# Counting the edges of a graph with the digit built on VectorE, eight one-hots kept, and TensorE's products in one written order

## The chip, the cores and the metric

The kernel runs on one core of one Trainium2 chip. A core has five engines that this text names: TensorE (PE), which multiplies matrices; VectorE (DVE), ScalarE (ACT) and GpSimd (POOL), which work on rows; and SyncE (SP), which here only issues transfers. Each runs its own queue of instructions in order, and semaphores join them. TensorE writes its sums to eight banks of PSUM; VectorE and ScalarE copy them out to SBUF, the memory in which the operands lie. The metric is the device time of one execution in microseconds (us).

## What is computed

The reference is a chain of four residual layers on 625 nodes of 512 features. Only the first is touched by the change: a graph convolution in hyperbolic space, done twice with two sets of weights. Cut to what matters:

```python
x = x + L0_gnn(layernorm(x), edge_index, W1, b1, W2, b2)   # this layer
x = x + L0_ffn(layernorm(x), ...)                           # eight experts, top 2
x = x + L1_gnn(layernorm(x), ...)                           # a second graph layer
x = x + L1_ffn(layernorm(x), ...)                           # memory attention, gated map

def gcn_conv(x, W, b, row, col, norm, n):
    h = mobius_matvec(W, x)              # x @ W.T, then scaled by its norms
    h = mobius_add(h, expmap0(b))
    t = logmap0(h)
    msg = norm[:, None] * t[row]
    agg = segment_sum(msg, col, num_segments=n)
    return expmap0(agg)                  # tanh(norm) * u / norm, kept inside the ball
```

There are 10,000 edges and a loop at each node. `norm` is the product of both ends' degrees to the power -0.5.

## The kernel before

The nodes are held as 5 tiles of 125 rows (`NT`, `P`). The sum over the edges is a product with a dense matrix AT of 625 x 625 counts, made once and used in both convolutions and again in the third layer.

**The count.** The 10,000 edges lie as 80 columns of 125. For each column VectorE compares the numbers 0 to 624 with the edges' senders (`sh`, L355, 125 x 625 in f16) and the numbers 0 to 374 with their receivers (`at_node`, L356, 125 x 375). A receiver of 375 or above is counted in the same 375 columns with a weight of 4096, so that one sum holds two digits. ScalarE multiplies that weight in (`dh`, L357). TensorE then adds `sh` times `dh` to five banks (`eps`, L361, five products a column; the fifth has a row of ones more, whose sums are the degrees). `sh` rotates over three tiles (`NSH`), `dh` over three, `at_node` over two. The function `count_edges` (L343 to L399) does this for a group of columns: 0 to 15 (`EARLY`), 16 to 47, 48 to 79 (`GROUP` is 32). At a group's end VectorE copies the degree sums (`total`, L370), TensorE turns them (`dps`, L373), ScalarE copies the five banks as integers (`both`, L386), and VectorE splits the digits (L390) and adds them to AT (L395; ScalarE writes the first group's, L393). The last group's degrees give `dis`, the root of their inverse.

**The nodes.** VectorE takes the statistics of x (L228, L231), ScalarE the root, and VectorE writes the normalised rows `u` (L244). The statistics are ordered behind the sixth column (`AHEAD`). ScalarE squares `u` for its norms (L255). In `conv_in` (L407) TensorE turns the weights (`wps`, L414) and `u` (`trps`, L265), ScalarE and VectorE copy these out (`WT` L415, `uT` L267 and L269), and TensorE makes five map tiles of 125 x 512 (`mxps`, L438). Of each tile ScalarE takes the squares (L440), VectorE the product with the bias row `yb` (L442), and ScalarE a copy (`raw`, L444). A chain of small operations on VectorE and ScalarE follows, with four changes of ScalarE's function table (L99), and at last a scaling of `raw` (L484, L485). `conv_out` (L488) scales by `dis` and makes the aggregation `agps` (L496, 25 products of 125 x 512), and so on for the second weights.

**What sets the order.** A scheduler at compile time places each engine's instructions by the order of the program and their expected readiness; tiles of a pool rotate over their buffers, and the eight banks are one pool (`psum`, L290) in this layer. `order(later, sooner)` (L187) puts one instruction behind another of its engine. `busy` (L193) issues fills: products of `full` with itself whose results nobody reads; there are 18 ahead of the second aggregation (L492) and 31 ahead of the first turn of the second layer's rows (`trps` at L568, in that layer's own pool of banks, L549). At the start SP, ACT and POOL each issue a part of the loads of indices, x, weights and bias; the first weights of the experts are issued on SP once the statistics have read x (`nodes_in`, L519, L630).

Of the kernel before, what the change touches and what calls it, by code (L numbers as in the profile page):

```python
# [16 lines left out]
F32 = mybir.dt.float32  # L17
# [32 lines left out]
EARLY = 16  # L50

AHEAD = 6

NSH = 3
# [4 lines left out]
def rows_of(ap, n):  # L59

    return bass.AP(tensor=ap.tensor, offset=ap.offset, ap=[[0, n], [1, ap.shape[-1]]])


class Rows:
# [42 lines left out]
    def artanh(self, out, z):  # L107
# [14 lines left out]
        self.chain(out, ln, 0.5, s, OP.mult, OP.add)  # L122
    def norm(self, n, inv, sq):

        self.act(n, sq, AF.Sqrt)
        self.at_least(n, n, EPS)
        self.inverse(inv, n)

    def expmap0(self, sq, name):
# [3 lines left out]
        n, inv = self.new("ex_n"), self.new("ex_inv")  # L133
        scale, inside = self.new(name + "_s"), self.new(name + "_n")
        self.norm(n, inv, sq)
# [7 lines left out]
def layers_kernel(  # L143
# [49 lines left out]
    def busy(ps, n, behind):  # L193

        for _ in range(n):
            filled = T.matmul(ps[:, :128], full, full, start=True, stop=True)
            order(filled, behind)
# [39 lines left out]
    def layernorm(y, extra=None, behind=None, pieces=((0, NT),)):  # L237
# [10 lines left out]
        return read  # L248
# [9 lines left out]
    def transposed(psum, to, y, c, scale=1.0, pieces=PIECES, wait=None):  # L258

        for a, b in pieces:  # L260
            ps = psum.tile([128, 512], F32, tag="ps", name="trps")
            if wait is not None and a == 0:
                busy(ps, *wait)
            for t in range(a, b):
                T.transpose(ps[:, (t - a) * P : (t - a + 1) * P], y[:, t, c * 128 : (c + 1) * 128], ident[:P, :P])  # L265
# [14 lines left out]
    with ExitStack() as es:  # L280
        big = spool(es, "l0big", 1)
        work = spool(es, "l0work", 2)
        hot = spool(es, "hot", 3)
# [29 lines left out]
        senders = [big.tile([P, N + 1], F16, name=f"sh_{i}") for i in range(NSH)]  # L313
# [29 lines left out]
        def count_edges(first, last):  # L343
# [5 lines left out]
            acc = [psum.tile([128, 512], F32, tag="ps", name="eps") for _ in range(NT)]  # L349
            rows_of_acc = [P] * (NT - 1) + [P + 1]  # L350
            for j in range(first, last):
                sh = senders[j % NSH]
                at_node = hot.tile([P, HALF], F16, tag="at", name="at_node", bufs=2)
                dh = hot.tile([P, HALF], F16, tag="dh", name="dh")
                V.tensor_scalar(sh[:, :N], nodes, src_f[:, j : j + 1], None, op0=OP.is_equal)  # L355
                built = V.tensor_scalar(at_node, nodes[:, :HALF], dst_f[:, j : j + 1], None, op0=OP.is_equal)  # L356
                A.activation(dh, at_node, AF.Copy, scale=weight[:, j : j + 1])  # L357
                if j == AHEAD - 1:
                    ahead.append(built)
                for i, n in enumerate(rows_of_acc):  # L360
                    T.matmul(acc[i][:n, :HALF], sh[:, i * P : i * P + n], dh, start=j == first, stop=j == last - 1)  # L361
            digits = ((0, HALF, OP.bitwise_and, DIGIT - 1), (HALF, N - HALF, OP.logical_shift_right, SHIFT))
            both = work.tile([P, NT, HALF], I32, tag="both", name="both", bufs=1)
            with ExitStack() as now:
                if last == EC:
                    now.enter_context(tc.high_priority())


                total = big.tile([128, NT * D], F32, tag="uT" if first else "raw", name="total")[: P + 1, :HALF]
                V.tensor_copy(total, acc[NT - 1][: P + 1, :HALF])  # L370
# [14 lines left out]
            for i in range(NT):  # L385
                A.activation(both[:, i, :], acc[i][:P, :HALF], AF.Copy)  # L386
# [20 lines left out]
        def conv_in(k, u, scale, inside, pieces, own=None):  # L407


# [6 lines left out]
            yb = work.tile([P, D], F32, tag="yb", name="yb", bufs=1)  # L416
            V.tensor_scalar(yb, b_row[k], b_scale[:, k : k + 1], None, op0=OP.mult)
            y2 = b_square[:, k : k + 1]

            uT = big.tile([128, NT * D], F32, tag="uT", name="uT")[:, : DC * N].rearrange("p (c n) -> p c n", n=N)  # L420
# [906 lines left out]
```

## Time and profile before

| | us |
|---|---|
| median of 3 runs (2324.1 to 2325.33) | 2324.68 |
| the profiled execution | 2322.8 |
| its span, from the first to the last instruction | 2320.8 |
| PE busy in the span | 2232.5 (96%) |
| VectorE busy | 1621.8 (70%) |
| ScalarE busy | 867.1 (37%) |
| first product of the count starts at | 5.88 |
| first product of the first map (L438) starts at | 43.99 |
| first product of the first aggregation (L496) starts at | 133.62 |
| first turn of the second layer's rows (L265) starts at | 222.84 |

Times are from the span's start. An engine that is busy for 96% of the whole span may still stand idle in a stage, so the table is to be read beside the windows that the prediction shows. A busy PE may also run at a granted clock below 1.00; the windows give that clock. The length that the profile gives for a short instruction has its latency in it: two instructions of VectorE that follow one another may start closer together than the length of the first, so starts are compared where a pace is meant. The profile's line numbers are those of the listing above.

### The profile page before, as it was taken

How to read it: one execution, taken by the hardware profiler on the slowest of the kernel's cores; microseconds unless marked ns; L12 is line 12 of the kernel's file. 1: busy time of each engine (PE TensorE's matmuls, PEld its weight loads, DVE VectorE, ACT ScalarE, POOL GpSimd, SP SyncE). 2: the span in 40 equal slices, each digit the busy share in tenths (PEclk: the TensorE clock that was granted, in tenths of full speed). 3: DMA queues.
4: the chain of work that ended last, by engine and by line, in shares of the span. 5: the costliest groups of instructions: out<-in, count | busy, mean ns of one | idle time of the engine just before them, and what ended most of it. 6: DMA issues, size and time to landing. Idle time of an engine off the chain costs nothing.

```text
span 2320.8 us, 34522 instructions
## 1 busy us (share of the span) xinstructions
PE 2232.5 (96%) x12794; PEld 1768.9 (76%) x12794; DVE 1621.8 (70%) x2303; ACT 867.1 (37%) x2867; POOL 991.9 (43%) x1058
## 2 busy tenths in 40 slices
PE   6898999999999999999999999999999999999987
PEld 4655866665788888888888888888888888888853
DVE  5744533332477788888778888778888877888782
ACT  6755211111243434433433443343443343344322
POOL 1000000020146555666555566655566655556531
PEclk8999999999999999999999999999999999999989
DMA  7000588863123322222322222332222232221110
GB/s 254 1 8 29 192 290 291 301 209 78 32 39 95 74 59 59 65 59 71 87 69 59 66 59 59 94 74 59 59 66 59 68 91 68 59 66 40 42 59 22
DMA packets 326025, 204.67 MB, mean 88 GB/s; under 512 B 275534, under 2 KB 279563, under 8 KB 321000
## 3 DMA queue, kind: packets, MB, share of 16 engines
q1 hardware_dynamic: 317371, 189.65, 27.7%
q10 hardware_dynamic: 3639, 7.56, 0.9%
q0 software_dynamic: 4848, 5.26, 0.8%
q8 instruction: 101, 1.65, 0.3%
q14 instruction: 66, 0.54, 0.1%
HBM read 197.18 MB, written 5.23 MB: 87 GB/s over the span
## 4 chain that ended last, share of the span: by engine, by line
PE 86%; ACT 5%; DVE 4%; POOL 2%; issue 2%; DMA 1%; POOLq 0%; ACTq 0%; SPq 0%; DVEq 0%
PE h1ps L1135 35%; PE scps L1036 19%; PE kbps L1023 5%; PE hps L737 5%; PE ops L748 5%; PE zps L1072 3%; POOL zsq L1079 2%; PE eps L361 2%; ACT zs L1075 2%; PE stps L831 2%; PE agps L496 2%; PE atps L1063 2%; PE l1ps L838 1%; PE mxps L438 1%; DVE hacc L1183 1%
## 5 line engine op out<-in xcount | busy, mean ns | idle before, releaser
L1147 DVE TENSOR_TENSOR hacc<-hacc,h1ps 128x942 f32<-128x942 f32 (+1 forms) x510 | 529.0, 1084 | 11.7 <-PE h1ps L1135 11.7
L1036 PE MATMUL scps<-keys,xnT 128*125 128x400 f32 x1280 | 435.1, 499 | 0.0
L1095 POOL TENSOR_TENSOR wq<-wz 128x256 f32<-128x256 f32 x248 | 241.1, 982 | 405.6 <-PE h1ps L1135 347.4
L1036 PEld LDWEIGHTS scps<-keys,xnT 128*125 128x125 f32 x1280 | 240.0, 188 | 185.0 <-issue 3.8
L1044 ACT ACTIVATE att<-att,a_top 125x100 f32<-125x100 f32 x640 | 232.0, 364 | 361.5 <-DVE a_top L1039 361.5
L1135 PE MATMUL h1ps<-zT,wq 128*128 128x157 f32 x1736 | 302.8, 296 | 0.0
L1135 PE MATMUL h1ps<-zq,wq 128*128 128x157 f32 x1736 | 302.7, 297 | 0.0
L1079 POOL TENSOR_TENSOR zsq<-zsq,zs 128x628 f32<-128x628 f32 x124 | 187.6, 1513 | 201.5 <-ACT zs L1075 201.5
L1135 PEld LDWEIGHTS h1ps<-zT,wq 128*128 128x128 f32 x1736 | 256.2, 190 | 0.0
L1135 PEld LDWEIGHTS h1ps<-zq,wq 128*128 128x128 f32 x1736 | 255.9, 190 | 0.0
L1066 ACT ACTIVATE attT<-atps 100x375 f32<-100x375 f32 (+1 forms) x256 | 92.5, 432 | 397.4 <-PE atps L1063 397.4
L1095 POOL TENSOR_TENSOR wq<-wz,wq 128x256 f32<-128x256 f32 x248 | 210.9, 850 | 19.4
L1076 DVE TENSOR_SCALAR zT<-zps,cols 128x628 f32<-128x628 f32 x128 | 111.6, 872 | 149.0 <-ACT zs L1075 147.6
L1055 ACT ACTIVATE att<-att,a_tot 125x100 f32<-125x100 f32 x620 | 170.2, 364 | 10.7 <-DVE a_tot L1045 10.7
L1072 PE MATMUL zps<-attT,vc 100*128 100x314 f32 x512 | 161.0, 436 | 10.6 <-ACT attT L1066 10.5
L1095 POOL TENSOR_TENSOR wq<-wsum,wq 128x256 f32<-128x256 f32 x186 | 161.5, 868 | 14.6
L1095 POOL TENSOR_TENSOR wq<-wsum 128x256 f32<-128x256 f32 x186 | 135.9, 731 | 65.0 <-PE h1ps L1135 65.0
L1135 PE MATMUL h1ps<-zT,wz 128*128 128x157 f32 x992 | 152.6, 296 | 0.0
L1014 DVE STREAM_TRANSPOSE wqT<-wqraw 128x512 f32<-128x512 f32 x128 | 80.2, 681 | 101.6 <-PE kbps L1023 82.5
L1135 PEld LDWEIGHTS h1ps<-zT,wz 128*128 128x128 f32 x992 | 141.0, 190 | 9.1
L1075 ACT ACTIVATE zs<-zps 128x628 f32<-128x628 f32 x128 | 88.7, 693 | 124.7 <-POOL zsq L1079 111.2
L1072 PEld LDWEIGHTS zps<-attT,vc 100*128 100x128 f32 x512 | 87.5, 191 | 45.9 <-ACT attT L1066 26.9
(400 smaller groups left out, 3487.3 us busy)
## 6 DMA issues: line engine op xcount, KB each, us to landing
w<-in_L_ffn_w_dram SPq DMA_DIRECT2D x16, 4096.0 KB
wz<-in_L_ffn_wz_w_dram SPq DMA_DIRECT2D x32, 2048.0 KB
wqraw<-in_L_ffn_Wq_w_dram SPq DMA_DIRECT2D x512, 64.0 KB
cb<-qbias SPq DMA_DIRECT2D x32, 195.3 KB
wkv<-in_L_ffn_Wkv_w_dram SPq DMA_DIRECT2D x1, 4096.0 KB
W_raw<-in_L_gnn_W_dram SPq DMA_DIRECT2D x2, 1024.0 KB
w<-in_L_ffn_Wkv_w_dram SPq DMA_DIRECT2D x1, 2048.0 KB
l1w<-in_L_gnn_W_dram SPq DMA_DIRECT2D x2, 1024.0 KB
```

The costliest lines, as they stand in the source:

```text
L737: T.matmul(ps[:, i * CAP : (i + 1) * CAP], w1[e][:, c, hc * 128 : (hc + 1) * 128], xgT[e][:, c, :], start=c == 0, stop=c == DC - 1)
L748: T.matmul(ps[:CAP], hT[e][:, hc, :], w2[e][:, hc, :], start=hc == 0, stop=hc == HC - 1)
L1023: folded.last = T.matmul(ps[:, k, h * L : (h + 1) * L], wqT[b][h][:, (c + k) * 128 : (c + k + 1) * 128], kcT[:, b * HB // H, :], start=Tru ...
L1036: T.matmul(ps[:P, t - t0, : HB * L], xnT[:, c, tp(t)], keys[b][:, c, :], start=c == 0, stop=c == DC - 1)
L1044: A.activation(own, own, AF.Exp, bias=top[:, t, h : h + 1], accum_out=tot[:, t, h : h + 1])
L1055: A.activation(own, own, AF.Copy, scale=tot[:, t, h : h + 1])
L1072: T.matmul(ps[:, u, : 2 * QN], vc[:, g * DH : (g + 1) * DH], attT[h % 2][:, 2 * u * QN : 2 * (u + 1) * QN], start=True, stop=True)
L1075: A.activation(zs, ps[:, :, : 2 * QN], AF.Square)
L1079: nc.gpsimd.tensor_tensor(zsq, zsq, zs.rearrange("p u s -> p (u s)"), op=OP.add)
L1095: engine.tensor_tensor(to, x, y, op=OP.subtract)
L1135: T.matmul(ps[:, at % 6 // 3, at % 3 * QN : (at % 3 + 1) * QN], now[j][:, m * 128 : (m + 1) * 128], zquarter[b][j][:, place[i]], start=Tru ...
L1147: V.tensor_tensor(to, to, got, op=OP.add)
```

## The change

The count is cut into three parts: `counting` takes the banks, `column` builds one column and issues its five products, `taken` copies a group's sums out, and `added` splits them and adds them to AT. In the new order of the program:

- The groups are columns 0 to 31, 32 to 63 and 64 to 79. Nine fills stand ahead of the first column.
- VectorE builds `dh` in one operation: the comparison, and the multiplication by the weight. `at_node` and ScalarE's part are gone. `sh` and `dh` rotate over eight tiles each (`HOT`).
- 18 columns (`EARLY`) come ahead of the nodes' work, and the statistics are ordered behind the twelfth (`AHEAD`).
- The other 14 columns of the first group come between the five tiles of the first map, three behind each.
- A group's sums are taken at its end and added behind the second column of the next; the turns of the small vectors (`colps`, `gtps`) move from behind the count into the second group.
- Through all of this `T` is a `Lane`: each product is ordered behind the one before it in the program, so TensorE keeps the written order.
- The norms of `u` come from its variance in two small operations on VectorE, in place of ScalarE's squares. The scale of the bias is carried by two small operations and `yb` is gone.
- `u`, `uT` and `raw` rotate over two buffers in place of one for each.
- The 31 fills move from the turn of the second layer's rows to the end of the second `conv_out`, behind its last product and in a bank of this layer.

The diff, cut to its core:

```diff
-EARLY = 16
-AHEAD = 6
-NSH = 3
+EARLY = 18
+AHEAD = 12
+HOT = 8
...
+class Lane:
+    def __init__(self, engine, order):
+        self.engine, self.order, self.last = engine, order, None
+    def _behind(self, op):
+        if self.last is not None:
+            self.order(op, self.last)
+        self.last = op
+        return op
+    def matmul(self, *args, **kinds):
+        return self._behind(self.engine.matmul(*args, **kinds))
...
-                at_node = hot.tile([P, HALF], F16, tag="at", name="at_node", bufs=2)
-                V.tensor_scalar(sh[:, :N], nodes, src_f[:, j : j + 1], None, op0=OP.is_equal)
-                built = V.tensor_scalar(at_node, nodes[:, :HALF], dst_f[:, j : j + 1], None, op0=OP.is_equal)
-                A.activation(dh, at_node, AF.Copy, scale=weight[:, j : j + 1])
+            V.tensor_scalar(sh[:, :N], nodes, src_f[:, j : j + 1], None, op0=OP.is_equal)
+            built = V.tensor_scalar(dh, nodes[:, :HALF], dst_f[:, j : j + 1], weight[:, j : j + 1],
+                                    op0=OP.is_equal, op1=OP.mult)
...
-                    V.scalar_tensor_tensor(junk, ps[:P], 1.0, yb, op0=OP.mult, op1=OP.mult,
+                    V.scalar_tensor_tensor(junk, ps[:P], 1.0, b_row[k], op0=OP.mult, op1=OP.mult,
                                            accum_out=dot[:, t : t + 1])
                     A.activation(raw[:, t, :], ps[:P], AF.Copy)
+                    if beside is not None:
+                        beside(t)
...
+            if last:
+                product = busy(psum.tile([128, 512], F32, tag="ps", name="spare"), 31, product)
...
-        count_edges(0, EARLY)
-        u = big.tile([P, NT, D], F32, tag="u", name="u", bufs=1)
-        nodes_in = layernorm(u, behind=ahead[0])
-        s, inside = RP[0, NT].expmap0(squares(work, u, "in_sq"), "ex")
+        T = Lane(nc.tensor, order)
+        group = counting(0, GROUP)
+        busy(group[2][0], 9, None)
+        for j in range(EARLY):
+            column(group, j)
+        u = rotating("u")[:P].rearrange("p (t n) -> p t n", n=D)
+        mv, nodes_in = layernorm(u, behind=ahead[0])
...
+        V.tensor_tensor(sq, mv[:, :, 1], layernorm.rs, op=OP.mult)
+        r.chain(sq, sq, float(D), layernorm.rs, OP.mult, OP.mult)
...
-        sent, mapped = conv_in(0, u, s, inside, ((0, NT),))
-        for first in range(EARLY, EC, GROUP):
-            count_edges(first, min(first + GROUP, EC))
+        turned = turned_in(0, u)
+        rest = iter(range(EARLY, GROUP))
+        def beside(t):
+            for j in range(3):
+                for c in rest:
+                    column(group, c)
+                    break
+        sent, mapped = conv_in(0, turned, s, inside, ((0, NT),), beside=beside)
+        for j in rest:
+            column(group, j)
+        sums = taken(group)
+        for first in range(GROUP, EC, GROUP):
+            last = min(first + GROUP, EC)
+            group = counting(first, last)
+            for j in range(first, last):
+                column(group, j)
+                if j == first + 1:
+                    added(sums)
+                if j == first + 8 and first == GROUP:
...
+            sums = taken(group)
+        added(sums)
+        T = nc.tensor
...
-                transposed(psum, xfT[:, c, :], xf, c, pieces=(piece,), wait=None if c else (31, product))
+                transposed(psum, xfT[:, c, :], xf, c, pieces=(piece,), wait=None if c else (0, product))
```

## The prediction, written before the result was known

> **What bounds the kernel now.** I read the windows of 5 us first (where TensorE, PE, stands still), then PE's timeline (what ended each gap), then the groups by form (the length of one instruction). Only the first layer, 0 to 225 us, is touched.
>
> Windows; columns: stretch and its length, busy time and count of PE, weight loads, VectorE, ScalarE (ACT), GpSimd, then PE's granted clock, DMA share, GB/s.
>
> ```profile
> 35.00:40.00 5.00, 0.54 (x3) 0.31 (x3) 3.02 (x20) 4.97 (x13) 0.00 (x0) 0.67 1.00 406
> 40.00:45.00 5.00, 1.69 (x3) 0.78 (x4) 1.87 (x9) 4.97 (x12) 0.00 (x0) 0.50 1.04 387
> 70.00:75.00 5.00, 1.22 (x7) 0.76 (x6) 4.02 (x22) 4.96 (x10) 0.00 (x0) 0.93 0.00 2
> 75.00:80.00 5.00, 3.30 (x11) 2.42 (x11) 4.02 (x10) 3.37 (x6) 0.00 (x0) 0.50 0.00 0
> 85.00:90.00 5.00, 5.00 (x34) 4.28 (x33) 3.78 (x13) 3.88 (x7) 0.00 (x0) 1.00 0.00 0
> ```
>
> From 35 to 45 and 70 to 75 us ACT is full and PE nearly empty; behind each hole PE runs at clock 0.50. From 85 to 90 PE itself is the limit.
>
> PE's timeline; columns: start, length, instructions, and in brackets the idle time before them with what ended it.
>
> ```profile
> 16.13 8.26 PE L361 MATMUL eps<-dh,sh 125*125 125x375 f16 x40 [5.18 <-DVE sh L355]
> 42.16 0.68 PE L265 MATMUL trps<-ident,u 125*128 125x125 f32 x2 [6.17 <-ACT WT L415]
> 43.99 18.90 PE L438 MATMUL mxps<-WT,uT 128*125 128x512 f32 x40 [1.15 <-ACT uT L267]
> 76.70 22.21 PE L361 MATMUL eps<-dh,sh 125*125 125x375 f16 x125 [4.12 <-ACT dh L357]
> 133.62 24.45 PE L496 MATMUL agps<-raw,AT 125*125 125x512 f32 x50
> 181.55 4.18 PE L196 MATMUL agps<-full 128*128 128x128 f32 x36
> 214.19 8.82 PE L196 MATMUL trps<-full 128*128 128x128 f32 x62 [5.89 <-DVE x L510]
> 222.84 2.30 PE L265 MATMUL trps<-ident,xf 125*128 125x125 f32 x20
> ```
>
> The stage that changes runs from the first edge product (5.88 us) to the first product of the first aggregation (133.62 us): 127.7 us. At full clock its PE work is 88.9: 80 columns of edges at 0.795 (from 112 to 127 us each column's build starts that far behind the last) 63.6; five map tiles at 3.43 (the starts of the square sums at 53.4 and 56.8) 17.2; 16 turns of weights 1.95; 20 turns of nodes at 0.125 2.5; degree products 3 x 0.68 = 2.0; the turns of small vectors some 1.6. The brackets from 5.88 to 133.62 add up to about 28 us of idle, and half clock behind them makes the other 10 or 11. So 38.8 us is the most that order can win here.
>
> **What the change removes and adds, part by part.**
>
> *One column.* Groups by form; columns: busy us, mean ns, idle before and its releaser.
>
> ```profile
> L357 ACT ACTIVATE dh<-at_node,weight 125x375 f16<-125x375 f16 x80 | 47.9, 608 | 27.5 <-PE eps L361 13.3 <-DVE at_node L356 13.1 <-DVE ln_st L228 1.0
> L355 DVE TENSOR_SCALAR sh<-nodes,src_f 125x625 f16<-125x625 f16 x80 | 30.6, 382 | 2.9 <-PE eps L361 2.7
> L356 DVE TENSOR_SCALAR at_node<-nodes,dst_f 125x375 f16<-125x375 f16 x80 | 25.3, 318 | 9.3 <-ACT dh L357 9.1
> ```
>
> The 47.9 us on ACT goes, and with it one handover per column. VectorE's two builds start 0.30 and 0.23 us behind one another when nothing holds them (4.58, 4.88, 5.10). The second now also multiplies by a per-row scalar. No row shows that form in f16. Lower bound: 0.23, the multiplication free. Upper bound: the two-input add of 375 f32 elements (L395), 0.46 from start to start. The nearest row is the two-scalar subtract-and-multiply of L244, 512 f32: 0.46 from start to start against 0.40 for the one-scalar L405, so the second scalar costs 0.06 and leaves the rate. I take 0.23 + 0.06 = 0.29, a column 0.59 (0.53 to 0.76), below PE's 0.795. VectorE stays ahead, by up to eight columns in place of three.
>
> *The start.* Nine fills (36 records of such fills take 4.18, so two records a fill: 2.1 us at full clock, twice that at half) run while the indices are loading, ahead of any column. Columns begin at 4.58 + 0.59 = 5.2, and 18 of them end on PE at about 5.2 + 18 x 0.795 = 19.5, where before VectorE stood in the first statistics, waiting for x until 14.50, with six columns built. Now 12 to 18 are built by then (4.58 + 18 x 0.59 = 15.2). The node chain: statistics and aggregates 5 x 0.75 from 15.4 to 19.2, root and reciprocal to 19.9 (one table load of 1.28 now lies in ACT's idle time), five rows of u at 0.46 to 22.2; before, 28.4. The squares of u on ACT (5 x 0.81) are replaced by two small VectorE operations and leave the path. PE turns W meanwhile (19.5 to 22; its load's traffic ends at about 21) and u at 22.2 + 2.5, with some 1.5 for three free banks and the last copy: the map starts at 26.3, before 43.99.
>
> *Map and columns.* In the written order five tiles and 14 columns follow one another: 17.2 + 11.1 = 28.3, end 54.6. ACT's three visits to a tile lie beside it; VectorE needs 14 x 0.59 + 5 x 0.69 = 11.7 of the 28.3 and builds eight columns ahead.
>
> *First group border.* Five banks hold sums, three rotate. The next group's fourth and fifth products need copies of `both` on ACT (0.39 each from start to start), but there the chain behind the map runs, with four table loads of 1.28; before, fillers on ACT got places in it at 66.75, 68.76, 71.08 and then 76.15. Lower bound: 0.5 (two copies at once); upper: 12, if the copies come behind the last scaling (3.06), with a cold clock. The nearest rows are the fillers at the first two places, 3.8 and 5.9 us behind the last map product; from the group's end at 54.6 that is 2 to 4. I take 4.0, with a part at half clock: 58.6.
>
> *The other 48 columns.* 32 x 0.795 + 0.7 + 1.2 (vector turns, now in midst of columns) = 27.3. VectorE has in this time the chain (some 4.5), its five scalings (3.4), digits, diagonal and degrees (4) and 24 to 32 columns (14 to 19): about as much as PE. I add 1.5 for columns that come late: 87.4. Second border, ACT free: 1.0. Then 16 columns, one set of degree products and 1.0 for the 6.6 us of digits and sums on VectorE: 12.7 + 0.7 + 1.0. End at 102.8. The last columns' end to the first aggregation was 133.62 - 129.03 = 4.6, with 0.45 of it a digit ahead of the degree copy, and vector turns in it that are now earlier: I take 4.1. First aggregation at 106.9, **26.7 us earlier**. It then starts as cold as before and costs the same 24.45. The edits of the bias (its scale carried by small operations, no `yb`) take 0.48 of VectorE off twice, covered by PE in both maps: nothing; uncovered, 0.5.
>
> *The last fills.* 31 fills waited for the residual's last read (5.89 idle), ran cold in 8.82, and kept PE until 222.84, though the normalised rows were there at 217.6 and 219.5. Put behind the last aggregation in a bank of the same layer, they run warm from 208.3 to 215.5 (62 x 0.116). The turns then end about 0.9 behind the last row, 220.4 to 220.7 in place of 225.07: **4.4 us**. Bounds: 0, if the two idle us make the clock fall and routing waits elsewhere, and 5.
>
> Queues: on SP the first expert loads wait for the last statistics (issued at 21.76, now about 19); no transfer is put ahead of another. The first three weight tiles were there by 52 us, long ahead of their use after 225, and later ones start when tiles come free, so the rest moves along with the layer.
>
> **Sum.** 26.7 + 4.4 = 31.1. The profiled execution took 2322.8 us (span 2320.8, 2.0 outside it): 2291.7. The median shown is 2324.68, so 1.9 more: **2293.6**.
>
> A row against a rule. From 30 to 32 us PE turned W and u at granted clock 1.00, behind 1.39 of idle. The Trainium skill (TensorE: Matmul & The Clock Gate, Part 4: PE-mode transpose) says that such turns do not count as busy to the clock. By that rule the map would start cold behind 5 us of turns; with the half window of 3.4 us that the page gives, an estimate of 1.7 us, it would be 2295.3. By the row it is 2293.6; the row decides.
>
> **Rivals.**
> *A: PE in one order waits behind ACT.* For it: four table loads in the chain and a filler as late as 76.15; one order means that no later column may pass. Against: fillers found earlier places. At its upper bound the border costs 12 + 2 for the cold clock in place of 4: 10 later, 2304; 0.17.
> *B: VectorE becomes the bound*, the second operation taking the 0.46 of L395. A column is 0.76; from 54.6 on VectorE needs 40 x 0.76 + 19.4 = 50, the first aggregation comes at 110, with the start 2 to 3 later 113: six later, 2300; 0.13.
> *C: slower.* The same second operation, far dearer. Some 58 columns lie on VectorE's path (18 before the map, 40 behind it), so each 0.1 us more in a column costs 5.8. B's 2300 is 25 below before; the sign turns at 0.76 + 25 / 58 = 1.19 for a column, 0.89 for the operation. At 1.0 for it the time is 2300 + 58 x 0.54 = 2331. For it: f16 with two scalars is not in the trace. Against: no VectorE row of 375 elements is above 0.55. 0.04.
> *D: the change does not do what it says*: the statistics come ahead of columns 12 to 17, and VectorE's queue holds back columns at the border, so that the gaps move and do not close. With 3 of the 31.1 left the time is 2322; 0.04.
>
> **How the numbers follow.** Forecast 0.62: 2293.6, A 0.17, B 0.13, C 0.04, D 0.04. Lower end: border at 0.5 and no late columns (5 us), tail and fills 2 better, 0.53 for a column (3 us): 2284. Upper end: A with the fills' gain at zero, 2304 + 4.4, and 2 for columns: 2311. A measurement tells 0.2% (4.6 us) from no change. Faster by more 0.92, within 0.04, slower 0.04.
>
> **What would show it.** In the profile after: no dh on ACT; the second build at a distance of 0.29; no clock under 0.9 between 10 and 95 us; the first mxps at about 26; the gap ahead of the 33rd column about 2 to 4 and its releaser `both`; first agps at about 107; fills at its end with no gap. I am wrong if the columns' pace is VectorE's (over 0.795 with PE waiting for dh), if one gap above 8 us stands at a border, or if stages behind 225 us do not simply come earlier.

## The result, and the profile after

The changed kernel took **2296.43 us** (median of 4 runs, 2293.93 to 2299.3), the kernel before 2325.01 beside it (4 runs, 2324.1 to 2326.89): ratio 0.9876, 95% interval 0.9859 to 0.9894, 28.6 us less. The forecast was 2293.6. The sum came out nearly right, but its largest term did not: the start of the map came 11 us late, and other terms gave part of that back. The profiled execution of the changed kernel is the slowest of the four; that of before is 2.2 us under the median beside it. The table therefore has a second profile of the changed kernel, from another execution (the first of the experiments).

| us from the span's start | before | forecast | after | after, again |
|---|---|---|---|---|
| the execution | 2322.8 | 2291.7 | 2299.3 | 2296.36 |
| span | 2320.8 | | 2297.5 | 2294.6 |
| first map product | 43.99 | 26.3 | 37.47 | 36.49 |
| from there to the first aggregation | 89.6 | 80.6 | 78.7 | 76.4 |
| first aggregation | 133.62 | 106.9 | 116.18 | 112.84 |
| from there to the routing product (`lps`) | 91.45 | 87.1 | 85.35 | 85.44 |
| `lps` | 225.07 | 194.0 | 201.53 | 198.28 |
| from there to the end of the span | 2095.7 | | 2096.0 | 2096.3 |

TensorE's timeline of the kernel after; columns: start, length, instructions, and in brackets the idle time before them with what ended it. L77 and L80 are the lines of `Lane`.

```profile
20.43 1.53 PE L80 MATMUL wps<-ident,W_raw 128*128 128x128 f32 x12
31.47 1.11 PE L80 MATMUL wps<-ident,W_raw 128*128 128x128 f32 x4 [9.52 <-ACT WT L461]
...
37.47 5.26 PE L77 MATMUL mxps<-WT,uT 128*125 128x512 f32 x8
...
44.96 3.60 PE L77 MATMUL mxps<-WT,uT 128*125 128x512 f32 x8
...
68.42 1.12 PE L77 MATMUL eps<-dh,sh 125*126 125x375 f16 x6 [0.16 <-ACT raw L494]
70.50 0.81 PE L77 MATMUL dps<-ident,total 126*125 126x1 f32 x6 [0.96 <-ACT both L408]
...
116.18 23.25 PE L548 MATMUL agps<-raw,AT 125*125 125x512 f32 x50 [2.45 <-DVE raw L450]
...
189.56 7.09 PE L221 MATMUL spare<-full 128*128 128x128 f32 x62
```

The brackets of 4 to 6 us that stood before the change are gone, and a single new one of 9.52 us stands ahead of the map. The 18 columns end at 20.4, the border shows 0.16 and 0.96, and the fills have no gap ahead of them. The first tile of the map takes 5.26 us and the second 3.60: the granted clock is 0.50 from 28 us on and until 40.8, so through most of the first tile.

Two windows of the same kernel (length, PE, weight loads, VectorE, ScalarE, GpSimd, clock, DMA share, GB/s):

```profile
25.00:30.00 5.00, 0.00 (x0) 0.00 (x0) 4.33 (x18) 1.68 (x5) 0.00 (x0) 0.72 1.03 425
...
85.00:90.00 5.00, 5.00 (x33) 4.29 (x32) 5.00 (x19) 0.00 (x0) 0.00 (x0) 1.00 0.00 0
```

From 25 to 30 us PE does nothing, where VectorE is nearly full. From 85 to 90 both are full and ScalarE, which had 3.88 us of work there before, has none.

Why PE waited 9.52 us is seen on ScalarE's timeline of the same kernel:

```profile
21.05 0.63 ACT L582 ACTIVATE junk<-b_row 125x512 f32<-125x512 f32 x1 [16.75 <-DMA b_row<-in_L_gnn_b_dram]
...
23.39 0.63 ACT L582 ACTIVATE junk<-b_row 125x512 f32<-125x512 f32 x1 [1.62 <-DMA b_row<-in_L_gnn_b_dram]
...
24.13 1.28 ACT L121 ACT_TABLE_LOAD   x1
25.43 0.21 ACT L121 ACTIVATE ln_rs<-ln_rs 125x5 f32<-125x5 f32 x1
...
29.02 0.21 ACT L121 ACTIVATE ex_n<-in_sq 125x5 f32<-125x5 f32 x1 [3.29 <-DVE in_sq L103]
...
30.84 1.55 ACT L461 ACTIVATE WT<-wps 128x512 f32<-128x512 f32 x3
```

Two squares of the bias rows, whose sums the map's products do not need, stand ahead of the root of the statistics (`ln_rs`) in ScalarE's queue, and their transfers land as late as 21 and 23.4 us. Behind them comes a table load of 1.28 us, which the prediction had put into ScalarE's idle time. VectorE had its part of `ln_rs` at 21.02 (L259); the root comes at 25.43. The copies of the turned weights (`WT`) stand behind both norms, the second of which waits for `in_sq`, itself made behind `u`, and behind a table load. With three free banks PE can turn 12 of 16 blocks and then stands still until the first of these copies, begun at 30.84, frees a bank; it goes on at 31.47. Before the change the root had stood ahead of the squares:

```profile
24.26 0.21 ACT L102 ACTIVATE ln_rs<-ln_rs 125x5 f32<-125x5 f32 x1
...
35.78 0.61 ACT L525 ACTIVATE junk<-b_row 125x512 f32<-125x512 f32 x1
```

The 0.7 us that the prediction gives to the root and the reciprocal hold no wait for the squares.

VectorE's timeline has the operation whose price was unknown:

```profile
4.71 0.37 DVE L390 TENSOR_SCALAR dh<-nodes,dst_f,weight 125x375 f16<-125x375 f16 x1
4.99 0.38 DVE L389 TENSOR_SCALAR sh<-nodes,src_f 125x625 f16<-125x625 f16 x1
5.29 0.37 DVE L390 TENSOR_SCALAR dh<-nodes,dst_f,weight 125x375 f16<-125x375 f16 x1
```

From the start of `dh` to that of the next `sh` it is 0.28 us here and 0.29 in most of the later columns, where 0.29 was forecast (0.23 before, without the second scalar). A column costs VectorE 0.58.

### The profile page after: what moved, and what is told of

The parts are those of the page before. It is cut to its first block, busy times and chain, and to the rows that moved or that the text cites. A ratio compares the mean times of both kernels' runs of the same rounds, so it can differ in the third digit from the quotient of the medians.

```text
span 2297.5 us, 34432 instructions
## 1 busy us (share of the span) xinstructions
PE 2230.4 (97%) x12812; PEld 1770.4 (77%) x12812; DVE 1618.5 (70%) x2303; ACT 814.8 (35%) x2773; POOL 991.4 (43%) x1063
## 3 DMA queue, kind: packets, MB, share of 16 engines
q0 software_dynamic: 4848, 5.26, 0.9%
## 4 chain that ended last, share of the span: by engine, by line
PE 86%; DVE 4%; ACT 4%; POOL 2%; issue 2%; DMA 1%; ACTq 0%; POOLq 0%; DVEq 0%
PE h1ps L1222 35%; PE scps L1123 19%; PE kbps L1110 5%; PE hps L824 5%; PE ops L835 5%; PE zps L1159 3%; POOL zsq L1166 2%; ACT zs L1162 2%; PE stps L918 2%; PE eps L77 2%; PE agps L548 2%; PE atps L1150 2%; PE l1ps L925 1%; DMA b_row<-in_L_gnn_b_dram 1%; DVE hacc L1270 1%
```

## The experiments

All ran in three groups of four, in the order of the table, each beside runs of the kernel before (medians 2325.43, 2325.27 and 2324.11). Ratios are to those, with 95% intervals; the last columns are from one profile of each. after_again stands in the first group only, so a difference of medians across groups has the groups' own in it (up to 1.3 us in the kernel before); the places within the profiles decide.

| run | median us | ratio | map starts | first aggregation | `lps` |
|---|---|---|---|---|---|
| after_again | 2297.31 | 0.9877 (0.9862 to 0.9892) | 36.49 | 112.84 | 198.28 |
| bias_late | 2292.67 | 0.9859 (0.9844 to 0.9874) | 32.91 | 111.87 | 197.96 |
| weights_first | 2293.24 | 0.9860 (0.9845 to 0.9875) | 32.71 | 110.97 | 196.47 |
| fills_only | 2316.38 | 0.9961 (0.9948 to 0.9975) | 44.47 | 134.38 | 220.93 |
| woven | 2283.74 | 0.9823 (0.9809 to 0.9836) | 34.62 | 101.40 | 186.89 |
| no_lane | 2292.76 | 0.9861 (0.9846 to 0.9876) | 37.28 | 112.60 | 198.79 |
| not_between | 2301.36 | 0.9901 (0.9886 to 0.9916) | 36.98 | 118.02 | 203.22 |
| digit_scalar | 2318.35 | 0.9970 (0.9958 to 0.9981) | 48.98 | 134.88 | 221.45 |
| digit_scalar_late | 2305.45 | 0.9919 (0.9905 to 0.9932) | 35.29 | 121.14 | 206.96 |
| three_hots | 2301.51 | 0.9899 (0.9883 to 0.9914) | 32.60 | 121.69 | 206.93 |
| digit_only | 2316.53 | 0.9966 (0.9953 to 0.9978) | 43.44 | 127.00 | 219.88 |
| woven_warm | 2282.71 | 0.9818 (0.9804 to 0.9831) | 34.61 | 101.40 | 185.19 |

The theory after the result: the change takes ScalarE out of the columns and lets columns fill the map's neighbourhood, and the order of ScalarE's queue costs about 10 us of it at the start. Rivals: the start is held by VectorE or by the transfers; or one part (the digit, the buffers, the written order) makes all of the gain.

**The changed kernel again**, with no edit.

> The changed kernel unaltered, timed beside its variants. Four executions so far lay in two pairs, 2294 and 2299 us, with a mean granted clock of 0.992 and 0.989. If the bias rows' landing (21.05 and 23.39 us in the profile) sets the pairs, the first map tile in a profile with clock 0.992 starts earlier than 37.47 us by about 4; if only the phase of the clock gate does, it starts at the same time and the cold stretches are shorter. Expected 2294 to 2299, map at 33 to 37.5, aggregation at 112 to 116.2.

2297.31 us (2293.47 to 2298.56). The wait for `WT` is there again (9.14 us). The first aggregation is 3.3 us earlier than in the first profile. The map starts 1.0 earlier; its first tile takes 3.60 us and not 5.26, and the 35 products behind the border 5.76 and not 7.44, the same instructions at another clock; and a wait of 1.02 for `dh` shows that the slower run had hidden. The bias rows landed at much the same times (their squares start at 21.20 and 23.24, and at 21.05 and 23.39 in the first profile), so their landing is not what sets the two executions apart; the clock is.

**The bias's squares behind the root.**

```diff
-            A.activation(junk, b_row[k], AF.Square, accum_out=b_sq[:, k : k + 1])
+            order(A.activation(junk, b_row[k], AF.Square, accum_out=b_sq[:, k : k + 1]), acts["last"])
```

> The changed kernel with ScalarE's squares of the two bias rows ordered behind the root of the rows' variance. Theory 1 (ScalarE's queue): the root ran at 25.43 only because the squares stood ahead of it and waited for the bias rows until 23.39; now it runs at about 21.3, u ends at about 24.5 in place of 28.5, and the copies of the turned weights come behind the squares at about 24.3 in place of 30.84; map at about 31.5, aggregation 5 to 6 us earlier, total about 2290. Theory 2 (the rest hides it: VectorE was full from 75 to 110 us, so an earlier map only makes later columns wait): map earlier, aggregation and total as in the changed kernel, within 1 us.

TensorE's timeline:

```profile
25.10 0.66 PE L80 MATMUL wps<-ident,W_raw 128*128 128x128 f32 x4 [2.39 <-ACT WT L461]
...
32.91 6.20 PE L77 MATMUL mxps<-WT,uT 128*125 128x512 f32 x8 [0.51 <-DVE uT L302]
```

The wait for `WT` falls from 9.14 to 2.39 us and the map starts 3.6 us earlier, so the queue's order did hold it. But the map starts cold: its first tile takes 6.20 us, 2.6 more than after_again's, and the first aggregation gains the other 1.0 us only. That is the place that theory 2 gave, but not its reason: the later columns wait no longer than in after_again (1.02 and 0.27 us). The median is 4.6 us lower; the two profiles differ by 3.1, and 2.8 of these lie behind `lps`, where nothing is changed (see the clock below).

**The turned weights ahead of the bias and the norms.** ScalarE's order: root, four copies of `WT`, squares of the bias, norms.

```diff
+        WT, copied = weights_in(0, acts["last"])
...
-            A.activation(junk, b_row[k], AF.Square, accum_out=b_sq[:, k : k + 1])
+            order(A.activation(junk, b_row[k], AF.Square, accum_out=b_sq[:, k : k + 1]), copied)
```

> The changed kernel with ScalarE's order set to: root, the four copies of the turned weights, the squares of the bias rows, then the norms. Theory 1: PE no longer stands 9.5 us before the last four weight turns, u ends at about 24.5, the map starts at about 28 and warm (first tile 3.4 in place of 5.05): aggregation 9 to 11 us earlier, at about 105.5, total about 2286. Theory 2 (VectorE hides it): aggregation at 113 or later, total 2293 or above.

The wait for `WT` is 0.72, but the map starts at 32.7, where 28 was expected, and cold (first tile 5.52 us); the first aggregation comes at 110.97, where 105.5 was expected. With the one wait gone another ends last, on TensorE's timeline of this run:

```profile
22.75 0.66 PE L80 MATMUL wps<-ident,W_raw 128*128 128x128 f32 x4 [0.72 <-ACT WT L461]
24.66 1.15 PE L80 MATMUL trps<-ident,u 125*128 125x125 f32 x3 [1.26 <-DVE u L271]
...
28.61 0.68 PE L80 MATMUL trps<-ident,u 125*128 125x125 f32 x2 [1.12 <-DVE uT L302]
29.80 1.30 PE L80 MATMUL trps<-ident,u 125*128 125x125 f32 x5 [0.51 <-DVE uT L302]
...
32.71 5.52 PE L77 MATMUL mxps<-WT,uT 128*125 128x512 f32 x8
```

The turns follow VectorE's rows of `u` and its copies `uT`, which stand among column builds in its queue, and PE has nothing else to do between them. My theory that the weights were all of it fell: the rival (VectorE holds the start) has about as much.

**Columns between the turns.** On top of the last edit: two columns behind the turned weights, one behind each of the eight groups of turns of `u`, the last four between the map's tiles; the bias and the norms behind the last copy of `uT`.

```diff
+            if between is not None:
+                between()
...
+        one()
+        one()
+        turned, copied = turned_in(WT, u, one)
...
+            squared = A.activation(junk, b_row[k], AF.Square, accum_out=b_sq[:, k : k + 1])
+            order(squared, copied)
+        acts["last"] = squared
```

> The changed kernel with the turned weights copied by ScalarE right behind the root of the statistics, ten of the 14 columns placed on TensorE between the turns of the weights and the eight groups of turns of the nodes, four left between the map's tiles, and the bias's squares and all norms behind the last copy of turned nodes. Theory (the hole from the 18th column to the map is waiting that columns can fill, and the half clock behind it goes with it): TensorE ends turns and ten columns at 20.4 + 4.4 + 8.0 = 32.8 us with a full clock, the first map tile takes 3.6 us and not 5.3, the map with four columns ends at 53.2, the first aggregation starts at 102 us, the time is 2284. Rival (VectorE's own order holds the turns back: the rows of u, its copies of turned nodes and the builds of columns stand in one queue): half of that is lost, the first aggregation starts at 106 to 108, the time is 2288 to 2291.

2283.74 us, the first aggregation at 101.40: the theory's 2284 and 102. Between the 18th column and the map, in TensorE's timeline:

```profile
20.96 2.27 PE L80 MATMUL wps<-ident,W_raw 128*128 128x128 f32 x16 [0.43 <-DMA W_raw<-in_L_gnn_W_dram]
...
24.66 0.98 PE L80 MATMUL trps<-ident,u 125*128 125x125 f32 x3
25.47 0.96 PE L77 MATMUL eps<-dh,sh 125*125 125x375 f16 x5
...
34.62 3.60 PE L77 MATMUL mxps<-WT,uT 128*125 128x512 f32 x8
```

The map starts 1.9 us later than in the run before it, but ten columns (8.0 us) are done by then and the clock is full. The rows of `u` are done no earlier (at 26.1, in the run before it at 26.3); PE has work beside them. This is 13.6 us faster than the changed kernel (2297.31). The edit also moves the bias and the norms; what that gives by itself was not run.

**The written order taken away.** `T` stays TensorE itself, with no `Lane`.

```diff
-        T = Lane(nc.tensor, order)
```

> The changed kernel with everything but the written order of TensorE's products: the scheduler places them. Theory (the order itself is worth something, mostly at the first group border and in the map): the scheduler leaves columns and map apart, a hole of 3 to 6 us comes back at a border or behind the map, the first aggregation starts 3 to 8 us later than 113 to 116, the time is 2300 to 2306. Rival (the digit on VectorE and the eight one-hots do it all, and any order is as good): within 2 us of the changed kernel, 2295 to 2299.

The theory fell. The first aggregation starts at 112.60 against 112.84 and `lps` at 198.79 against 198.28: the written order is worth nothing here. The scheduler put columns between the turns by itself and had a gap of 2.14 us later. The lower median (2292.76) is no gain of this edit: the profiled span is 1.8 us shorter than after_again's, 2.3 shorter behind `lps` and 0.5 longer ahead of it.

**The 14 columns behind the map** in place of between its tiles.

```diff
-        sent, mapped = conv_in(0, turned, s, inside, ((0, NT),), beside=beside)
+        sent, mapped = conv_in(0, turned, s, inside, ((0, NT),))
```

> The changed kernel with the 14 columns behind the map's five tiles in place of between them. Theory (TensorE is the bound there, so that only its sum counts, and three banks let two tiles run ahead of ScalarE's two visits of about 1.3 us to a tile of 3.4): the map with the columns takes the same 29 to 31 us, the time is within 2 us of the changed kernel; the chain behind the map starts 10 us earlier, so the copies of the sums at the first border find ScalarE free, which may give up to 1. Rival (the place between the tiles covers something: the tiles' reads on ScalarE and VectorE): TensorE waits 0.5 to 1 us for each of three tiles, 2 to 4 us slower.

Both theories missed the place. The five tiles take their 17.3 us without a wait, but at the border TensorE waits 3.58 us for `both`, and then runs cold; the first aggregation is 5.2 us later than after_again's, the time 4.1 us longer. ScalarE's timeline shows who stands ahead:

```profile
65.02 0.47 ACT L408 ACTIVATE both<-eps 125x375 int32<-125x375 f32 x1
66.08 3.17 ACT L536 ACTIVATE raw<-raw,cv_k 125x512 f32<-125x512 f32 x5 [0.60 <-DVE cv_k L93]
69.16 1.57 ACT L408 ACTIVATE both<-eps 125x375 int32<-125x375 f32 x4
```

Four of the five copies of sums come behind the five scalings that end the map's chain. This is the prediction's rival A, at 3.6 us and not at its upper bound of 12. In the changed kernel the columns between the tiles put the group's end right behind the map's last tile, and the copies fall into the chain's gaps (in after_again two start at 64.38, one at 67.34 and two at 69.22, and the five scalings at 75.50).

**The digit on ScalarE again**, eight buffers and the rest kept.

```diff
+            at_node = hot.tile([P, HALF], F16, tag="at", name="at_node", bufs=2)
...
-            built = V.tensor_scalar(dh, nodes[:, :HALF], dst_f[:, j : j + 1], weight[:, j : j + 1],
-                                    op0=OP.is_equal, op1=OP.mult)
+            built = V.tensor_scalar(at_node, nodes[:, :HALF], dst_f[:, j : j + 1], None, op0=OP.is_equal)
+            A.activation(dh, at_node, AF.Copy, scale=weight[:, j : j + 1])
```

> The changed kernel with the digit scaled on ScalarE again, as before the change, eight buffers and the written order kept. Theory of the prediction (ScalarE's 80 scalings of 0.6 us and their handover were what held TensorE in the early columns, in the first statistics and beside the chain of the map with its four table loads): 18 columns end 2 us later, the copies of turned weights and nodes come later by 3 scalings or so, and at the first border 4 to 8 us are lost; the first aggregation starts 8 to 14 us later, the time is 2305 to 2311. Rival (the eight buffers alone carry TensorE over ScalarE's busy stretches, since 0.6 is below 0.795): 2297 to 2300.

2318.35 us, well over both. The squares of the bias now stand ahead of the scalings too. ScalarE's timeline:

```profile
20.26 0.63 ACT L583 ACTIVATE junk<-b_row 125x512 f32<-125x512 f32 x1 [16.34 <-DMA b_row<-in_L_gnn_b_dram]
...
22.17 0.63 ACT L583 ACTIVATE junk<-b_row 125x512 f32<-125x512 f32 x1 [1.18 <-DMA b_row<-in_L_gnn_b_dram]
...
22.80 6.47 ACT L392 ACTIVATE dh<-at_node,weight 125x375 f16<-125x375 f16 x12
```

TensorE waits 18.14 us for the first `dh`, until 23.4. The run mixes two costs, so the edit was made again on top of bias_late.

> The changed kernel with the digit scaled on ScalarE as before the change, and the squares of the bias ordered behind the root of the statistics, so that they no longer stand ahead of the scalings (that hole was 18.1 us in the run without this). To be held against the changed kernel with the same order of the bias (first aggregation at 111.9, 2292.7 us). Theory (ScalarE's scalings cost TensorE time by themselves, mostly behind the map, where four table loads and the scalings of the map stand in the same queue; in the run without the order, map start to first aggregation took 85.9 us and not 76.4): the first aggregation starts 8 to 13 us later, at 120 to 125, the time is 2301 to 2306. Rival (0.6 us for a scaling is below TensorE's 0.795 for a column, and eight buffers carry it over the rest, so that all of the loss was the bias's place): 2293 to 2296.

2305.45 us, 12.8 above bias_late; the first aggregation 9.3 us later. From the map's start to it 85.9 us go by and not 79.0, with a wait of 4.56 for `dh` at 80.8 and waits for `both` and `raw` of 2.6 in sum at the border; the wait for `WT` ahead of the map is 6.84 and not 2.39. (The two profiles differ by 11.3, of which 2.3 lie behind `lps`, where nothing is changed.) ScalarE's timeline at the longest wait behind the border:

```profile
76.53 3.17 ACT L537 ACTIVATE raw<-raw,cv_k 125x512 f32<-125x512 f32 x5 [1.11 <-DVE cv_k L93]
79.60 0.61 ACT L439 ACTIVATE AT<-digit 125x500 f32<-125x500 int32 x1
80.11 1.09 ACT L392 ACTIVATE dh<-at_node,weight 125x375 f16<-125x375 f16 x2
```

The theory holds: the scalings cost time by themselves, below TensorE's pace though each one is, because they stand in one queue behind the longer work of the map's chain.

**Three one-hots** in place of eight.

```diff
-HOT = 8
+HOT = 3
```

> The changed kernel with three one-hots kept in place of eight. Theory (VectorE builds a column in 0.58, faster than TensorE's 0.795, but stands still for columns when it does the statistics, the digits, the chain behind the map; eight buffers are 6.4 us of work for TensorE, three are 2.4): TensorE loses about 2 us in the first statistics, 2 to 4 behind the map and 1 to 2 in the digits of the second border; the first aggregation starts 4 to 8 us later than 113 to 116, the time is 2300 to 2306. Rival (small operations of VectorE are scattered among the builds, so that no stretch is longer than three columns): within 2 us of 2297.

2301.51 us, 4.2 more than the changed kernel. Its map starts 3.9 us earlier than after_again's (here the copies of `WT` came ahead of the second norm), yet the first aggregation is 8.9 us later: TensorE waits for `dh` six times, 8.3 us in all (1.3 with eight), mostly where VectorE has the chain behind the map, digits and scalings of rows. So the five buffers more are worth 7 us of waiting and some half clock behind it. (From the map's start to the first aggregation it is 89.1 us and not 76.4.) The time shows less of it than the place: the two profiles differ by 6.2 us, because 2.5 us are won behind `lps`, where nothing is changed.

**The digit alone**, in the kernel before: one operation for two, three buffers, the old order.

```diff
-                at_node = hot.tile([P, HALF], F16, tag="at", name="at_node", bufs=2)
...
-                built = V.tensor_scalar(at_node, nodes[:, :HALF], dst_f[:, j : j + 1], None, op0=OP.is_equal)
-                A.activation(dh, at_node, AF.Copy, scale=weight[:, j : j + 1])
+                built = V.tensor_scalar(dh, nodes[:, :HALF], dst_f[:, j : j + 1], weight[:, j : j + 1],
+                                        op0=OP.is_equal, op1=OP.mult)
```

> The kernel before the change with one edit: the digit built by one VectorE operation with two per-row scalars, three buffers and the old order kept. Theory (the digit's move alone takes ScalarE's waits out of the columns, 1.2 + 1.1 + 1.4 + 4.1 us at 67 to 77 us and some 2 us at 103 to 109, and the half clock behind them, but neither the wait for the first statistics (5.2) nor the wait for the copies of turned weights (6.2)): the first aggregation starts 7 to 12 us earlier than 133.6, the time is 2311 to 2318. Rival (without the new order VectorE becomes what the columns wait for, and the gaps only change their name): 2320 to 2326.

2316.53 us, 7.6 less than before, and the first aggregation 6.6 earlier, a little under the 7 to 12 expected. The waits that the theory left in place are there: 3.96 for VectorE in the first statistics and 5.22 for `WT`. In part the gaps did change their name, as the rival has it: where TensorE had waited 4.12 us for ScalarE's `dh` at 76.7, it now waits 2.73 for VectorE at 78.6. A good quarter of the gain, then, needs no new order.

**The fills alone**, moved in the kernel before.

```diff
+            if last:
+                product = busy(psum.tile([128, 512], F32, tag="ps", name="spare"), 31, product)
...
-                transposed(psum, xfT[:, c, :], xf, c, pieces=(piece,), wait=None if c else (31, product))
+                transposed(psum, xfT[:, c, :], xf, c, pieces=(piece,), wait=None if c else (0, product))
```

> The kernel before with one part of the change alone: the 31 fills at the end of the second aggregation. My prediction gave this part 4.4 us: first turn of the second layer's rows at about 217.6, lps at 220.6, total about 2320.5. Rival: the next layer's start is set by VectorE and the part gives nothing, total within 1 us of before.

2316.38 us, 9 less where 4.4 were expected. In its place the edit gives what was forecast: `lps` starts 4.1 us earlier, though the aggregation had started 0.8 later, so 4.9. Another 2.2 us lie behind `lps`, and 2.6 are the distance of before's profiled execution from the median beside it. Most of what lies behind `lps` in this pair is clock. TensorE's timeline at the start of the last layer's products, before and then with the fills moved:

```profile
587.65 4.63 PE L265 MATMUL trps<-ident,y 125*128 125x125 f32 x20 [0.87 <-DVE y L873]
592.08 4.89 PE L883 MATMUL hps<-xnT,kmap 128*100 128x375 f32 x16
```

```profile
583.51 3.43 PE L268 MATMUL trps<-ident,y 125*128 125x125 f32 x20 [0.88 <-DVE y L881]
586.78 4.38 PE L891 MATMUL hps<-xnT,kmap 128*100 128x375 f32 x16
```

Up to here the two are equal: the turns start 362.58 us behind `lps` in both. The turns then take 4.63 and 3.43 us and the products behind them 4.89 and 4.38; the granted clock is 0.73 over the turns and 0.89 over the products in the first, and 1.00 over both in the second. From the first of these turns to the end of the products that is 1.7 of the 2.2 us; the rest comes mostly in the last 100 us and was not followed. Over all kernels here the time from `lps` to the end lies between 2093.4 and 2096.3 us with the same code.

**Fills ahead of the first aggregation**, on top of the woven version.

```diff
+        busy(psum.tile([128, 512], F32, tag="ps", name="warm"), 9, None)
```

> The version with columns between the turns (2283.7 us), with nine fills of TensorE behind the last products of degrees, ahead of the first aggregation. Theory (the aggregation starts at a half clock, because TensorE is idle for 1.1 and 2.5 us ahead of it: 23.4 us for work that takes 21.7 at full clock): nine fills of 0.23 us fill the gap, the aggregation takes 21.7 to 22.3, the time is 2282.0 to 2283. Rival (the first gap of 1.1 us is enough for the half clock, or the fills run into the time at which the first rows are ready): the same within 0.5, or up to 1 slower.

The aggregation takes 21.69 us and not 23.39 (the granted clock from 102 to 104 us is 1.00 and not 0.50), and everything up to `lps` comes 1.7 earlier (185.19). The median is 2282.71; its ratio's interval overlaps the woven version's, so the profile shows this gain and the medians do not. It is the fastest version tried: 0.9818 of before, 41.4 us less.

Not run by themselves were the norms from the variance, the bias's scale without `yb`, the statistics behind the twelfth column, and the second buffers of `u`, `uT` and `raw`.

## Why the prediction was right in sum and wrong in a step

- **What order can win.** 38.8 us of idle and half clock were named as the bound up to the first aggregation. The change got 17.4 to 20.8 of it, the woven version 32.2. The bound held.
- **One column.** Right: 0.29 for the operation, 0.58 for a column. Rivals B and C needed 0.46 and 0.89.
- **The start: the step that failed.** The prediction let the map start at 26.3; it started at 37.47. The statistics ended 1.8 us later than said (21.02). The root and reciprocal took 4.8 us and not 0.7, because ScalarE's queue held two operations that wait for a transfer. From the end of `u` (28.4) to the map it was 9.1 us and not 4.1, with the copies of `WT` behind both norms, and PE's turns at a half clock. bias_late and weights_first show both orders as causes, but of a part only: with both mended the map starts at 32.7, 3.8 earlier than after_again's and still 6.4 later than forecast. There the statistics end 2.6 us later than said (21.81 for 19.2), because six columns are built between them in VectorE's queue; the reciprocal stands behind column builds too and comes at 23.62, although the root was there at 22.2; and from the last row of `u` (26.3) to the map it is 6.4 and not 4.1. The prediction added the nodes' small operations up one behind the other and gave nothing for the columns that stand between them in the same queue. woven shows what the stage can do: not the removal of the latencies but columns placed beside them.
- **Map and columns.** 28.3 forecast, 29.1 in after_again (36.49 to 65.6), where the clock is full. That placing the columns there was also what keeps the border short was not in the working; not_between shows it.
- **First border and the other 48 columns.** 48.2 forecast, 42.9 measured in after_again (65.6 to the last column's end at 108.5). The border was 1.1 and not 4.0; rival A (0.17) did not come, and not_between has it, at 3.6. The allowances for a second border and for digits on VectorE, 1.0 each, were not needed; late columns were put at 1.5 and cost 1.3. This is what gave back half of what the start had lost (10.2 us in that profile).
- **First aggregation.** 26.7 earlier was forecast, 17.4 and 20.8 measured in two profiles. It also took 1.2 us less than the 24.45 that it was put at.
- **Fills.** 4.4 forecast, 4.9 measured.
- **The written order.** The prediction took it as part of the cause; no_lane shows no effect in its place.
- **The row against the rule.** The row, turns at clock 1.00 behind 1.39 us of idle, did not come again: 9.1 to 9.5 us of idle stood ahead of the turns, and they began at 0.50. In the first profile the map then started cold, in after_again not (5.26 and 3.60 us for its first tile). That 2295.3, the time by the rule, lies nearer to the result than 2293.6 decides nothing.
- **The signs that were named.** No `dh` on ScalarE, the distance of the second build and the fills without a gap came true. The clock did not stay above 0.9 (0.50 from 28 to 40.8 and from 72 to 74 us), the first map product was not at 26, and the one gap above 8 us stood ahead of the map and not at a border.
- **The result against the median.** The two profiles have `lps` 23.5 and 26.8 us earlier, 31.1 was forecast; the medians differ by 28.6. The profiled execution of before was 2.2 us faster than the median beside the result, which makes up the rest for the second profile. That the forecast missed the time by 2.8 us only is in part luck: up to `lps` the terms of after_again are off by 10.2 and 0.8 late, 5.3 early, 0.2 late and 1.6 early, which leaves 4.3; and the 1.9 us that the prediction adds from the profiled execution to the median, and that the changed kernel's second profile did not have (2296.36 against 2296.43), covered part of that.

## What to carry to other kernels

An instruction that waits for a transfer holds all that stands behind it in its engine's queue, and a change elsewhere can let the scheduler put it ahead of one that is urgent: for each step on the path, read the queue of the engine that does it, in the new kernel and not in the old. Where TensorE waits for the latency of small work on other engines, place independent products in the gaps, one by one, before trying to shorten the latency: mending the queue brought `lps` forward by 1.8 us (4.1 in the medians), filling the gaps by 9.6 more (9.5). And when a stage is moved, ask which of its neighbours relied on where it stood, as the copies at the border did.

## What the runs showed of the hardware

- **A second per-row scalar** in an f16 VectorE operation of 125 x 375 adds 0.05 to 0.06 us (0.23 to 0.28 or 0.29 from start to start).
- **The same hole does not always cost the same.** The executions of the changed kernel lie between 2293.5 and 2299.3 us; in its two profiles the hole at the first border costs a half clock in the one (0.50 from 72 to 74 us) and none in the other (1.00 throughout). In after_again the clock came back during the turns themselves. The windows of TensorE in that run (length, busy time and count, granted clock, DMA share, GB/s); from 32 to 36 us PE does nothing but turns:

```profile
32.00:33.00 1.00, 1.00 (x7) 0.50 1.06 442
33.00:34.00 1.00, 1.00 (x7) 0.50 1.01 418
34.00:35.00 1.00, 0.81 (x7) 0.88 1.06 442
35.00:36.00 1.00, 0.49 (x3) 1.00 0.94 393
```

The clock is full again some 3 us after the turns begin at 31.3. In the first profile of the same kernel the turns begin at 31.5 and the clock stays at 0.50 until 40.8. The Trainium skill (TensorE: Matmul & The Clock Gate, Part 4: PE-mode transpose) says that such turns do not count as busy in the same way; after_again speaks against it. So do not_between and digit_scalar_late, where the clock came back 3.5 to 4 us after the turns had begun (granted 0.70 from 35 to 36 us with turns from 31.6, and 0.80 from 33 to 34 with turns from 29.9). three_hots stands with the first profile: its turns run from 26.0 to 31.0 without a wait and on to 32.6, and the clock falls to 0.50 in the first microsecond of them and stays there until 36.8. What makes the difference between these executions was not settled.
